# A transformer block on one core: a beta moved from VectorE to GpSimd, TensorE given idle transposes during the first load, and a new order of work

## The chip, the cores and the metric

The kernel runs on one core of a Trainium2 chip. Its engines are TensorE (PE; its weight loads are shown as PEld), VectorE (DVE), ScalarE (ACT), GpSimd (POOL) and SyncE (SP), which issues the DMAs. Times are device microseconds of one execution; the number to predict is the median over several executions.

## The reference

`x` holds 8 batches of 512 rows of 256 floats (fp32), `ctx` 64 rows per batch. Per batch:

```
y = ln0(x)                                        # no gain, no shift
y = ln(y + attention(y, y, y, causal), g1, beta1)
y = ln(y + attention(y, ctx, ctx),     g2, beta2)
h = relu(y @ w1 + b1)                             # 256 -> 1024
y = ln(y + h @ w2 + b2,                g3, beta3)
x = x + y
q = fp4(ln0(x))                                   # blocks of 16 quantised and scaled back
h = silu(q @ fp4(w_gate).T) * (q @ fp4(w_up).T)   # 256 -> 704
x = x + fp4(h) @ fp4(w_down).T
```

Keys and queries are the rows themselves; there are no projections. `beta3` is one row of 256 floats, added to all rows in the third norm. Since x + (norm * g3 + beta3) = (x + beta3) + norm * g3, it may be added to x at any time after `ln0(x)` has been taken.

## The kernel before, in words

Rows lie on the 128 partitions, so a batch is four row tiles of 128x256. All matmuls are fp32. Each stage of a batch is built from small operations that name an engine, a cost, the buffers they read and write, and what they emit (`Plan.op`, line 118). Nothing is emitted at once. At the end (L1171) `Plan.order` runs a list scheduler: every engine that is free takes the ready operation with the smallest key, provided that the buffers it needs can be had, and the instructions are emitted in that order. So each engine gets one fixed queue, worked off first to last, and an instruction whose input is late holds up all behind it.

The key comes from `_keys` (L153): the due time of the operation's batch and stage (the table `DUE`, L45) less the costs of what follows it. `push` shifts a key: `LOAD_EARLY` (L44) pulls the loads of x and z forward, and the weights (L1163) are pushed back. Costs and dues are constants in the file; what they say is only the planner's, and it acts on the chip through the order alone. The number of buffers of each kind (L310 to L347) also shapes the order.

Stages, with the lines whose instructions matter below:

- `load` (L349): x of a batch (L358, four DMAs for batch 0, else one of 512 KB) and z, that is `ctx`, twice (L366).
- `self_attention` (L747): `norm_stats` takes row statistics on VectorE (L448, L438, L439), 1/sqrt on GpSimd as a power (L458) and a shift on VectorE (L465); `layernorm` writes y on ScalarE, a row tile each (L524); `turned` transposes y on TensorE (L419) in two halves that ScalarE copies out of PSUM (L831); scores on TensorE (L767: for each of four key tiles two products, 512, 384, 256 and 128 columns wide); exp on ScalarE (L778); the causal mask as a select on GpSimd (L787); values on TensorE (L800); division on VectorE (L806, L807). `scaled_norm` (L531) takes squares on ScalarE (L488), the power on GpSimd (L503), gain and shift on VectorE (L537, L545).
- `cross_attention` (L860): z transposed (L419, copied at L867 into `zT`), the batch's result `r` transposed (L419, L831), keys (L883) copied as `kq` (L896) and transposed back (L900), exp (L890), values (L927).
- `mlp` (L947): up products (L961) with relu (L969), down products (L981). `by_row` (L552, its instruction at L557) adds `b2` to r and `beta3` to x on VectorE, four instructions of 128x256 each.
- `glu` (L1019): fp4 on VectorE and ScalarE (L578 to L610), gate and up products (L1036), down products (L1116), result stored (L1133).
- `columns` (L724) loads `b1` as eight rows, `c_rows`, which TensorE transposes (L733), and seven vectors spread over all partitions by DMA (L743). `pads` (L1146) stores a tile of zeros, `nothing`, into three DRAM buffers (L1149).

Before the plan begins, GpSimd makes the identity `ident` and fills the constant parts of 2 `y0`, 8 `z` and 3 `hqT` buffers and `nothing` (L374 to L388).

Of the kernel before, what the change touches and what calls it, by code (L numbers as in the profile page):

```python
# [14 lines left out]
ALU = mybir.AluOpType  # L15
# [23 lines left out]
TURN = 2.6  # L39

TILED = 2.65

BY_PRODUCTS = (4, 2, 1)
LOAD_EARLY = 2191.0  # L44
DUE = [  # L45
    [-1877.0, 638.0, 1236.0, -86.0, 359.0],
    [-498.0, 1140.0, 299.0, -53.0, 352.0],
    [251.0, 920.0, -109.0, 452.0, 665.0],
    [2244.0, 599.0, -92.0, 754.0, 95.0],
    [1032.0, 759.0, 1302.0, 1127.0, 22.0],  # L50
    [818.0, -579.0, 119.0, -1108.0, 586.0],
    [771.0, -1583.0, 341.0, 621.0, 85.0],
    [127.0, -388.0, -430.0, -94.0, -1479.0],
    [-2334.0],
]
# [205 lines left out]
def kernel(  # L261
# [51 lines left out]

    z_homes = several("z", 8, [P, D + 2])
    plan.kind("y0", y0_homes)
    plan.kind("z", z_homes)
    plan.kind("zT", several("zT", 6, [P, ND, SZ]))
    plan.kind("turned", several("turned", 3, [P, ND, S]), ordered=False)
    plan.share("y0T", "turned", 1)
    plan.share("yT", "turned", 3, ordered=False)  # L320
    plan.share("zqT", "turned", 3)
    plan.kind("e", several("e", 1, [P, NT * (NT + 1) // 2 * P]))
    plan.kind("r", several("r", 3, [P, NT, D]))
    plan.kind("kq", several("kq", 4, [P, S // 2]))
    plan.kind("xp", several("xp", 6, [P, NT, SZ]))
    plan.kind("xpT", several("xpT", 3, [P, NT // 2 * P]))
    plan.kind("hT", several("hT", 8, [P, S]))
    plan.kind("zq", several("zq", 1, [P, NT, D]))
    plan.kind("zm", several("zm", 2, [P, NT * D]), ordered=False)
    plan.kind("wide", several("h", 8, [P, NI * P]), ordered=False)  # L330
    plan.share("h", "wide", 5)
    plan.share("hm", "wide", 3)
    plan.share("wq", "wide", 7)
    hqT_homes = several("hqT", 3, [P, NI * P])
# [7 lines left out]
    plan.kind("zd", zd_homes, ordered=False)  # L342
    plan.kind("ln", several("ln", 12, [P, 48]), ordered=False)
    plan.kind("q", several("q", 6, [P, 3, 64]), ordered=False)
    plan.kind("rt", several("rt", 7, [P, 4]), ordered=False)
# [3 lines left out]
    def load(b):  # L349
        xs, zs = plan.buf("x"), plan.buf("z")  # L350
        plan.batch, plan.stage = b, 0
        plan.push = -LOAD_EARLY

        for ts_ in [[t] for t in range(NT)] if not b else [list(range(NT))]:
            lo, n = ts_[0], len(ts_)
            plan.op(
                "SP", 0.65 * n,
                lambda lo=lo, n=n: nc.sync.dma_start(  # L358
                    xs.ap[:, lo : lo + n, :],
                    x[b, lo * P : (lo + n) * P].rearrange("(t p) d -> p t d", p=P),  # L360
                ),
                writes=[(xs, t) for t in ts_],
            )
        for i in range(2):
            plan.op(
                "SP", 0.4, lambda i=i: nc.sync.dma_start(zs.ap[ts(i, SZ), :D], z[b]),  # L366
                writes=[(zs, i)],
            )
        plan.push = 0.0
        return xs, zs  # L370
# [3 lines left out]
    make_identity(nc, ident)  # L374
    for t in y0_homes:
        nc.gpsimd.memset(t[..., D:], 1.0)
    for t in z_homes:
        nc.gpsimd.memset(t[:, D:], 1.0)

    for t in hqT_homes:  # L380
        nc.gpsimd.memset(t[RI:, WI * P :], 0.0)
    squares = fixed("squares", [P, D])
    mhalf = fixed("mhalf", [P, NT])
# [3 lines left out]
    nothing = fixed("nothing", [P, 2, NI * P - I], U16)  # L387
    nc.gpsimd.memset(nothing, 0)  # L388

# [14 lines left out]

    plan.kind("const", ["const"] * 13, ordered=False)
    ready = {}
    for name in ("cols", "g1", "beta1", "g2", "g3", "beta2", "beta3", "b2", "w1", "w2", "wgu", "wd", "pads"):
        ready[name] = plan.buf("const")


    def transposed(blocks, src, dst, emit_evict, cost, width, also=()):

        pt = plan.buf("bank")

        def go():
            at = 0
            for blk in blocks():
                rows, n = blk.shape
                nc.tensor.transpose(pt.ap[:n, ds(at, rows)], blk, ident[:rows, :rows])  # L419
                at += rows  # L420

        plan.op("PE", 0.112 * width, go, reads=src, writes=[pt], takes=[dst[0]])
        plan.op("ACT", cost, lambda: emit_evict(pt.ap), reads=[pt, *also], writes=[dst])

    def norm_stats(v, view, pairs):
# [18 lines left out]
        for ts_ in pairs:  # L444
            lo, hi = ts_[0], ts_[-1] + 1
            for t in ts_:
# [9 lines left out]
            plan.op(  # L456
                "POOL", 1.05,
                lambda lo=lo, hi=hi: nc.gpsimd.tensor_tensor(  # L458
# [16 lines left out]
    def sums_stats(v, view, s):  # L475
# [9 lines left out]
        for t in range(NT):  # L485
            plan.op(
                "ACT", 0.52,
                lambda t=t: nc.scalar.activation(  # L488
                    squares, view(t), AF.Square, bias=s.ap[:, 24 + t : 25 + t],
                    accum_out=s.ap[:, 28 + t : 29 + t],  # L490
                ),
                reads=[(v, t), (s, t)], writes=[(s, ("sq", t))],
            )
# [7 lines left out]
        plan.op(  # L501
            "POOL", 1.05,
            lambda: nc.gpsimd.tensor_tensor(s.ap[:, 36:40], s.ap[:, 32:36], mhalf, ALU.pow),  # L503
            reads=[(s, "var")], writes=[(s, ("rstd", t)) for t in range(NT)],
        )

    def layernorm(dst, dview, v, view, s=None, pairs=(range(NT),)):

        if s is None:
            s = norm_stats(v, view, [list(ts_) for ts_ in pairs])  # L510
        else:
# [8 lines left out]
            )  # L520
        for t in range(NT):
            plan.op(
# [224 lines left out]
    def self_attention(b, xs):  # L747
# [4 lines left out]
            y0, lambda t: y0.ap[:, t, :D], xs, lambda t: xs.ap[:, t, :],  # L752
            pairs=(range(NT),) if b else (range(NT // 2), range(NT // 2, NT)),
        )
        yT = turned(y0, "y0T", b < BY_PRODUCTS[0], lambda t: y0.ap[:, t, :D])


# [3 lines left out]
        for k in range(NT):  # L761
# [3 lines left out]
            def scores(k=k, n=n, sc=sc):  # L765
# [19 lines left out]
            plan.op(  # L785
                "POOL", 0.35,
                lambda k=k: nc.gpsimd.affine_select(  # L787
# [7 lines left out]
        for t in range(NT):  # L795
# [9 lines left out]
            def divide(t=t, av=av, rt=rt):  # L805
# [7 lines left out]
                "PE", (t + 1) * pe(D + 2), product,  # L813
                reads=[(e, k) for k in range(t + 1)] + [(y0, k) for k in range(t + 1)],
                writes=[av], takes=[r],
# [6 lines left out]

    def turned(v, kind, by_products, view):

        yT = plan.buf(kind)
        if by_products:
            for c in range(ND):
                transposed(
                    lambda c=c: [view(t)[:, ts(c, P)] for t in range(NT)],
                    [(v, t) for t in range(NT)], (yT, c),  # L830
                    lambda pt, c=c: nc.scalar.copy(yT.ap[:, c, :], pt), act(S), NT,  # L831
                )
        else:
            turned_by_transfers(v, view, plan.buf("zm"), yT)
        return yT
# [111 lines left out]
    def mlp(b, r, xs):  # L947
# [5 lines left out]
        by_row(r, "b2", ALU.add)  # L953
        by_row(xs, "beta3", ALU.add)
        hT = []
        for f in range(NF):
            hp, h = plan.buf("bank"), plan.buf("hT")

            def product(f=f, hp=hp):
# [7 lines left out]
            plan.op(  # L967
                "ACT", act(S, True),
                lambda f=f, hp=hp, h=h: nc.scalar.activation(  # L969
# [49 lines left out]
    def glu(b, xs, s):  # L1019
# [91 lines left out]
        def last(t, hqT):  # L1111
            op = plan.buf("bank")

            def product(hqT=hqT, op=op):
# [6 lines left out]
            plan.op(  # L1121
                "PE", NI * pe(D), product, reads=[(hqT, 0), (hqT, 1), ready["wd"]], writes=[op]
            )
# [26 lines left out]


    columns()
    plan.op("SP", 3.5, pads, writes=[ready["pads"]])
    plan.batch = 0
# [7 lines left out]
    )  # L1162
    plan.push = 2035.0  # L1163
    weights()
# [40 lines left out]
```

## Time and profile before

| | us |
|---|---|
| median of 3 runs | 575.14 (575.07 to 575.2) |
| the profiled execution | 576.26 |
| its span, first to last instruction | 574.5 |
| TensorE matmuls busy | 563.8 |
| VectorE busy | 447.8 |
| ScalarE busy | 361.8 |
| GpSimd busy | 62.2, 93 instructions |

In the profile an fp32 matmul is two instructions, and a transpose is one. An instruction's duration includes the time it takes to drain, so in a full TensorE queue the step from one start to the next is shorter than the mean duration: 13.73 us for 32 L961 instructions, 0.43 each, whose mean duration is 0.59. For GpSimd, durations are rough. The chain that ended last is followed back from the last instruction, at each step to what released it. The granted TensorE clock is 1.00 in every stretch.

VectorE's 32 instructions that add `beta3` take 0.420 us each, 12.3 us busy in all. On GpSimd the 32 L503 powers take 1.18 us on average, 1.01 where nothing else disturbs them, and 32 selects 0.29 at the median, 1.68 at most.

### The profile page before, as it was taken

What the parts mean: (1) busy time and instruction counts of PE and PEld (TensorE: products, weight loads), DVE (VectorE), ACT (ScalarE), POOL (GpSimd) and SP (SyncE); (2) the same over time, 40 slices, a digit from 0 to 9 for tenths busy, and PEclk for the clock granted to TensorE, in tenths of its full rate; (3) what the DMA queues carried; (4) which work ended last, traced back from release to release, by engine and by line L of the source; (5) the groups of instructions that cost most, each with busy time, mean ns of one, the idle gap of its engine ahead of it and who ended that gap; (6) DMA issues with size and microseconds to landing.
All of it is one profiled execution on the core that took longest, in us unless ns stands there. A gap on an engine that the chain in (4) does not pass through costs nothing.

```text
span 574.5 us, 7037 instructions
## 1 busy us (share of the span) xinstructions
PE 563.8 (98%) x2209; PEld 391.2 (68%) x2209; DVE 447.8 (78%) x1125; ACT 361.8 (63%) x761; POOL 62.2 (11%) x93
## 2 busy tenths in 40 slices
PE   5999999999999999999999999999999999999997
PEld 2767584866747668658486667766765866877686
DVE  4789988869998865755259999978997656399892
ACT  4677869598887672791638558887845256364431
POOL 3521101011200120110101102210100000010000
PEclk9999999999999999999999999999999999999999
DMA  7770387246466513322023546585771421436501
GB/s 236 119 230 2 101 219 169 73 119 157 116 158 175 137 52 83 99 71 49 1 73 98 137 126 156 148 198 154 153 180 62 124 62 38 111 106 151 151 19 46
DMA packets 143220, 66.88 MB, mean 116 GB/s; under 512 B 107976, under 2 KB 142672, under 8 KB 143184
## 3 DMA queue, kind: packets, MB, share of 16 engines
q1 hardware_dynamic: 143184, 66.44, 45.4%
q8 instruction: 17, 0.28, 0.2%
q14 instruction: 19, 0.16, 0.1%
HBM read 10.42 MB, written 29.66 MB: 70 GB/s over the span
## 4 chain that ended last, share of the span: by engine, by line
PE 98%; ACT 1%; DMA 0%; SPq 0%; issue 0%; DVE 0%; ACTq 0%
PE bank L1036 27%; PE bank L981 19%; PE bank L961 19%; PE bank L1116 15%; PE bank L767 7%; PE bank L800 6%; PE bank L419 2%; PE bank L927 1%; PE bank L883 1%; DMA z<-in_ctx_dram 0%; ACT squares L488 0%; PE bank L900 0%; SPq L358 0%; ACT turned L831 0%; PE bank L1102 0%
## 5 line engine op out<-in xcount | busy, mean ns | idle before, releaser
L1036 PE MATMUL bank<-wgu,turned 128*128 128x352 f32 x512 | 157.5, 460 | 0.0
L1036 PEld LDWEIGHTS bank<-wgu,turned 128*128 128x128 f32 x512 | 96.3, 190 | 51.8 <-issue 1.7
L981 PE MATMUL bank<-w,hT 128*128 128x256 f32 x512 | 112.6, 379 | 0.0
L961 PE MATMUL bank<-turned,w 128*128 128x512 f32 x256 | 112.5, 593 | 0.0
L981 PEld LDWEIGHTS bank<-w,hT 128*128 128x128 f32 x512 | 97.0, 190 | 13.8
L1116 PE MATMUL bank<-wd,hqT 128*128 128x256 f32 x384 | 87.2, 380 | 0.0
L961 PEld LDWEIGHTS bank<-turned,w 128*128 128x128 f32 x256 | 48.2, 190 | 56.9 <-issue 51.7
L1116 PEld LDWEIGHTS bank<-wd,hqT 128*128 128x128 f32 x384 | 72.4, 190 | 14.2 <-issue 2.9
L503 POOL TENSOR_TENSOR ln<-ln,mhalf 128x4 f32<-128x4 f32 x32 | 37.7, 1180 | 352.0 <-DVE ln L496 352.0
L603 DVE SCALAR_TENSOR_TENSOR h<-h,h 128x704 f32<-128x704 f32 (+2 forms) x76 | 66.8, 883 | 3.8 <-ACT h L597 3.4
L488 ACT ACTIVATE squares<-r,ln 128x256 f32<-128x256 f32 x96 | 48.7, 508 | 32.0 <-DVE ln L480 29.7
L969 ACT ACTIVATE hT<-bank,cols 128x512 f32<-128x512 f32 x64 | 42.8, 681 | 21.7 <-PE bank L961 21.5
L1048 ACT ACTIVATE h<-bank 128x352 f32<-128x352 f32 x64 | 29.2, 460 | 36.4 <-PE bank L1036 32.5
L1071 ACT COPY h<-h 128x1408 uint16<-128x1408 uint16 x28 | 38.0, 1362 | 19.4 <-DVE h L610 17.9
L1055 DVE TENSOR_TENSOR h<-h,bank 128x352 f32<-128x352 f32 x64 | 32.4, 516 | 12.3 <-PE bank L1036 8.6
L992 DVE SCALAR_TENSOR_TENSOR r<-bank,r 128x256 f32<-128x256 f32 x32 | 13.5, 421 | 35.0 <-PE bank L981 34.7
L767 PE MATMUL bank<-turned 128*128 128x512 f32 (+3 forms) x128 | 39.8, 457 | 0.4 <-ACT turned L831 0.4
L597 ACT ACTIVATE h<-h 128x704 f32<-128x704 f32 (+2 forms) x38 | 29.7, 788 | 14.0 <-DVE h L591 13.9
L800 PE MATMUL bank<-y,e 128*128 128x258 f32 x160 | 36.8, 381 | 0.0
L800 PEld LDWEIGHTS bank<-y,e 128*128 128x128 f32 x160 | 30.1, 190 | 5.9 <-issue 1.0
L591 DVE SCALAR_TENSOR_TENSOR h<-h,q 128x704 f32<-128x704 f32 (+2 forms) x38 | 33.5, 883 | 0.2
L610 DVE TENSOR_TENSOR h<-h,q 128x704 f32<-128x704 f32 (+2 forms) x38 | 33.4, 879 | 0.2
(90 smaller groups left out, 639.9 us busy)
## 6 DMA issues: line engine op xcount, KB each, us to landing
zd<-zm SPq DMA_DIRECT2D x25, 512.0 KB, 3.0
hd<-h SPq DMA_DIRECT2D x30, 352.0 KB, 3.0
out_dram<-x SPq DMA_DIRECT2D x32, 128.0 KB, 1.7
x<-in_x_dram SPq DMA_DIRECT2D x7, 512.0 KB, 5.3
w<-in_L_xattn_w_dram SPq DMA_DIRECT2D x2, 1024.0 KB, 7.4
z<-in_ctx_dram SPq DMA_DIRECT2D x16, 64.0 KB, 4.6
zd<-h SPq DMA_DIRECT2D x2, 384.0 KB, 3.1
h<-in_L_ffn_w_down_dram SPq DMA_DIRECT2D x2, 352.0 KB, 4.2
```

The lines of the kernel that those rows point to most:

```text
L488: lambda t=t: nc.scalar.activation(squares, view(t), AF.Square, bias=s.ap[:, 24 + t : 25 + t], accum_out=s.ap[:, 28 + t : 29 + t],),
L503: lambda: nc.gpsimd.tensor_tensor(s.ap[:, 36:40], s.ap[:, 32:36], mhalf, ALU.pow),
L591: lambda: nc.vector.scalar_tensor_tensor(blocks_of(view()), blocks_of(view()), TIE, each(rc()), ALU.mult, ALU.mult),
L603: lambda reverse=reverse, f=f: nc.vector.scalar_tensor_tensor(view(), mm(), LEAST, view(), ALU.max, f, reverse1=reverse),
L767: nc.tensor.matmul(sc.ap[:, :n], yT.ap[:, c, ts(k, P)], yT.ap[:, c, k * P :], start=(c == 0), stop=(c == ND - 1),)
L800: nc.tensor.matmul(av.ap[:, : D + 2], e.ap[:, ds(start[k] + (t - k) * P, P)], y0.ap[:, k, :], start=(k == 0), stop=(k == t),)
L961: nc.tensor.matmul(hp.ap, w1_sb[:, c, ts(f, P)], yT.ap[:, c, :], start=(c == 0), stop=(c == ND - 1),)
L969: lambda f=f, hp=hp, h=h: nc.scalar.activation(h.ap, hp.ap, AF.Relu, bias=b1_sb[:, f : f + 1]),
L981: nc.tensor.matmul(fp.ap[:, :D], hT[f].ap[:, ts(t, P)], w2_sb[:, f, :], start=(f == 0), stop=(f == NF - 1),)
L1036: nc.tensor.matmul(gp.ap[:, :HI], zT.ap[:, c, ts(t, P)], wgu[:, c, ds(j * I + n * HI, HI)], start=(c == 0), stop=(c == ND - 1),)
L1071: lambda: nc.scalar.copy(planes(), h.ap[:, :I].bitcast(U16).rearrange("p (k h) -> p h k", h=2)),
L1116: nc.tensor.matmul(op.ap[:, :D], hqT.ap[:, ts(c, P)], wd[:, c, :], start=(c == 0), stop=(c == NI - 1),)
```

## The change

- **beta3**: `by_row(xs, "beta3")` on VectorE becomes four GpSimd instructions per batch on the same data.
- **Idle transposes**: 22 transposes of `ident` into a PSUM bank that nobody reads, first in TensorE's queue.
- **First rows on two engines**: for batch 0, y's row tiles 1 and 3 are written by VectorE (`tensor_scalar`), tiles 0 and 2 by ScalarE, and the second half of the transposed y is copied out of PSUM by VectorE.
- **Fills late**: only the first `y0` and the first `z` buffer are filled at once. The other fills and `nothing` become planned GpSimd operations with a late key, and their readers wait for them.
- **Durations**: the planner's costs of the power (1.05 to 1.12), the square (0.52 to 0.63), the select (0.35 to 0.44) and the relu (0.68 to 0.57) change.
- **Dues anew**: the table of dues, `LOAD_EARLY`, the push of the weights and the counts of some buffers (`kq` 4 to 1, `xp` 6 to 3, `xpT` 3 to 9, `hT` 8 to 9, `z` 8 to 9 and others) change.

```diff
-LOAD_EARLY = 2191.0
+LOAD_EARLY = 1813.0
 DUE = [
-    [-1877.0, 638.0, 1236.0, -86.0, 359.0],
+    [-1960.0, 1449.0, 703.0, -221.0, -105.0],
...
+    fills = [(of_y0, y0_homes[1:]), (of_z, z_homes[1:]), (of_hqT, hqT_homes)]
+    of_y0(y0_homes[0])
+    of_z(z_homes[0])
...
+        for t in on_dve:
+            plan.op(
+                "DVE", 0.35,
+                lambda t=t: nc.vector.tensor_scalar(
+                    dview(t), view(t), s.ap[:, 36 + t : 37 + t], s.ap[:, 40 + t : 41 + t],
+                    ALU.mult, ALU.add,
+                ),
...
-                    lambda pt, c=c: nc.scalar.copy(yT.ap[:, c, :], pt), act(S), NT,
+                    lambda pt, c=c: (
+                        nc.vector.tensor_copy(yT.ap[:, c, :], pt)
+                        if first and c
+                        else nc.scalar.copy(yT.ap[:, c, :], pt)
+                    ),
+                    act(S), NT, engine="DVE" if first and c else "ACT",
...
-        by_row(xs, "beta3", ALU.add)
+        for t in range(NT):
+            plan.op(
+                "POOL", 0.75,
+                lambda t=t: nc.gpsimd.tensor_tensor(
+                    xs.ap[:, t, :], xs.ap[:, t, :], vecs["beta3"][0], ALU.add
+                ),
+                reads=[(xs, t), ready["beta3"]], writes=[(xs, t)],
+            )
...
+    idle = plan.buf("bank")
+    def warm():
+        for _ in range(WARM):
+            nc.tensor.transpose(idle.ap[:, :P], ident, ident)
+    plan.op("PE", 0.22 * WARM, warm, writes=[idle])
     columns()
-    plan.op("SP", 3.5, pads, writes=[ready["pads"]])
+    plan.push = 2333.0
+    plan.op(
+        "POOL", 0.2, lambda: nc.gpsimd.memset(nothing, 0), writes=[(ready["fills"], "nothing")]
+    )
+    for fill, homes in fills:
+        for k, t in enumerate(homes):
+            plan.op(
+                "POOL", 0.45, lambda fill=fill, t=t: fill(t), writes=[(ready["fills"], (fill, k))]
+            )
...
-    plan.push = 2035.0
+    plan.push = 2333.0
     weights()
```

## The prediction

> **What bounds the kernel now.** I read the busy shares first, then the chain that ended last, then its first 60 us in order of time, then GpSimd's own timeline, then two-microsecond windows for the DMA rate. The page:
>
> ```profile
> PE 563.8 (98%) x2209; PEld 391.2 (68%) x2209; DVE 447.8 (78%) x1125; ACT 361.8 (63%) x761; POOL 62.2 (11%) x93
> PE 98%; ACT 1%; DMA 0%; SPq 0%; issue 0%; DVE 0%; ACTq 0%
> ```
>
> The first row is busy time, the second the chain by engine: TensorE is the bound. The view of waits gives it only 5.6, 0.9, 0.7 and 0.4 us of waiting, all before 36.9 us. So what can be won lies in the first 37 us. The chain there (start, length, what):
>
> ```profile
> 2.66 2.77 DMA z<-in_ctx_dram
> ...
> 8.33 1.74 PE bank L419 x7
> 10.06 6.71 PE bank L767 x16
> 16.78 4.36 PE bank L800 x20
> 21.14 1.14 PE bank L419 x10
> 22.28 4.11 PE bank L767 x12
> 26.39 0.15 PE bank L733
> 26.54 0.64 PE bank L767 x4
> 27.18 4.59 PE bank L800 x20
> 31.77 0.45 PE bank L419 x4
> ...
> 36.85 1.99 PE bank L767 x4
> ```
>
> The same 16 score matmuls cost 6.71 us for batch 0 and 4.11 + 0.64 = 4.75 for batch 1: half speed at the start, about 2 us lost. Transposes show it too: 1.74 / 7 = 0.25 us at 8.33, 0.45 / 4 = 0.11 at 31.77. Between 31.77 and 36.85 TensorE waits for ScalarE (squares, `kq`, `turned`).
>
> **The start: idle transposes, rows on two engines.** 22 transposes of `ident` begin when it is made (about 1.45 us) and cost 22 x 0.21 = 4.7 us cold, to 6.2. The z transposes, at 5.56 before, now come behind them, and ScalarE's `zT` copy, which stands ahead of y's rows in its queue, too: row 0 starts near 6.95 instead of 6.21. ScalarE then has two rows (2 x 0.52) instead of four, and VectorE the other two (0.42 each, from the 0.42 of a L557 row), so rows end at 8.05 instead of 8.27. Scores could start at about 9.4 instead of 10.0. VectorE's copy of the second half stands behind the statistics of batch 1's x, which wait for that x: it landed at 8.9 (the statistics start at 8.91) and they take 1.41, so 10.3 + 0.6 = 10.9. Cold, the first half's matmuls cover that (9.4 + 1.7 = 11.1).
>
> Does the clock come up? The row: half speed lasts till about 14.4 (the weight loads of L767 step by 0.85 us up to 13.57; ten of them fit into the 2.4 us after 14.21), 4.4 us after the first matmul at 9.99, though transposes ran without a pause from 8.33, which is 6.1 us earlier. The Trainium skill, "TensorE: Matmul & The Clock Gate", Part 4, says that transposes don't count as activity for the gate, and Part 1 that full speed comes about 4 us into sustained matmuls. Were transposes counted, 12.3 would have been expected. Row and rule speak against the warm-up. By the rule, batch 0's scores are cold again and its value products (L800) start at 9.4 + 6.7 + 0.15 + 0.22 = 16.5 instead of 16.78, as the transpose of `c_rows` and those of batch 1's z now stand between scores and values. If transposes count, scores wait for VectorE's copy at 10.9, run 3.5 us warm, and L800 starts at 14.9. I take 16.5.
>
> **Fills late.** The memsets (0.1 to 0.2 us each) run in GpSimd's idle time before its first power and between the first two. Nothing waits; 0. Dearest: one 0.2 in front of a power.
>
> **The queue of SP.** In the built order the three pad stores move up to right behind batch 1's x, and the seven vectors (g1 to beta3) ahead of x of batches 3 to 5 and of batch 2's z, whose transposes stand in front of batch 1's scores. The pads' own wait for the fill `nothing` ends before SP reaches them (about 1.6 against 4.5 us). Before, the vectors were on the way from 17 us on, and nobody waited for them:
>
> ```profile
> 18.00:20.00 2.00, 2.00 (x11) 1.74 (x10) 1.84 (x9) 0.56 (x2) 0.43 (x1) 1.00 0.76 136
> 20.00:22.00 2.00, 2.00 (x15) 1.65 (x14) 1.91 (x10) 0.39 (x1) 0.00 (x0) 1.00 0.87 129
> 22.00:24.00 2.00, 2.00 (x7) 1.00 (x7) 1.90 (x14) 1.94 (x7) 0.43 (x1) 1.00 1.34 78
> 24.00:26.00 2.00, 2.00 (x8) 1.33 (x7) 0.74 (x4) 1.97 (x7) 2.00 (x3) 1.00 0.65 99
> ```
>
> The last number is GB/s. The vectors are 7 x 131 = 917 KB; 2 us x (136 + 129 + 78 + 99) = 884 KB by 26, so they take some 8.3 us, far under the 315 GB/s of x at 10 to 12 us. Now they start when batch 2's x has landed: 8.9, pads and z about 1, 524 KB at 315 = 1.7, its late issue 1: near 12.5. So beta3 lands at about 12.5 + 8.3 + 0.5 for the last completion = 21.3 and that z just behind it (19 if the slow pace was the neighbours' fault). Batch 1's transposes end at 16.5 + 4.36 + 0.9 = 21.75 cold, 20.1 warm: z costs nothing cold and eats 1.4 warm. Scores of batch 1: 22.1 against 22.28. Batches 3 to 5 land near 27 instead of 17, still ahead of their readers but for one statistics instruction of batch 3, which waits in VectorE's queue till 23.6, before the squares are done.
>
> **beta3 on GpSimd.** VectorE loses 32 x 0.42 = 13.4 us; as TensorE never waits for VectorE after 37 us, that is worth 0. GpSimd gains 32 adds of 128x256. No row shows one. Below: a select of 128 columns with one input takes 0.29; twice the columns, 0.58. Above: GpSimd held up by VectorE:
>
> ```profile
> 25.53 1.01 POOL L503 TENSOR_TENSOR ln<-ln,mhalf 128x4 f32<-128x4 f32 x1
> 26.50 1.89 POOL L787 TENSOR_SCALAR_AFFINE_SELECT e<-e 128x128 f32<-128x128 f32 x4
> ...
> 40.14 1.68 POOL L787 TENSOR_SCALAR_AFFINE_SELECT e<-e 128x128 f32<-128x128 f32 x1 [2.53 <-ACT e L778]
> ```
>
> At 40.14 a 0.29 us select takes 1.68, beside seven L557 adds on VectorE. The skill's "SBUF — State Buffer", "Who interferes with whom", says either side may block, since a VectorE instruction with two SBUF inputs shares a read port with GpSimd; here VectorE's own L557 stay at 0.42, so by the row VectorE keeps its gain and GpSimd pays; by the rule VectorE could give back up to 32 x 0.58 = 19 us, which its 22% idle time covers. I take 0.85 for an add (the price in "GPSIMD Engine Reference", 3.1, 4.5 us for 2048 columns, is 0.56 plus dispatch, an estimate), bounds 0.58 to 1.7.
>
> What is queued behind them? GpSimd's order becomes: four selects of batch 0, a power, **six adds, which wait for beta3**, batch 0's power (`rstd`), then the selects of batch 1, which L800 of batch 1 waits for. Adds: 21.4 + 6 x 0.85 + 0.1 = 26.6; power 1.0; select 0.3: L800 of batch 1 starts at 27.95, against 27.18. At 0.58 the adds end at 25.0, the power then waits for ScalarE's squares (25.5) and L800 starts near 27.0: -0.2. At 1.3 it starts at 30.6: +3.4. I take +0.8.
>
> **The order on ScalarE and the rest of the dues.** After batch 0's `r` transposes, the copies ahead of `kq` grow by one `turned` (0.53) and two `zT` (0.45): `kq`'s transposes 5.4 us behind the `r` transposes instead of 4.4. The scores of batch 2 follow at 5.65 instead of 5.24, since their `turned` is copied earlier: +0.4. The 0.15 wait of the `r` transposes near 39.1 goes: more matmuls now stand ahead of them. From there both orders hold the same TensorE work. Followed by hand to batch 0's first L961, the new order shows no further wait; beyond it I take 0, up to 2 in places where a power stands behind adds, below -0.2 excluded, as TensorE has no waiting left to lose. The tail (3.2 us) is the same. The planner's four new durations and the buffer counts act through this order alone.
>
> **Sum.** +0.8 + 0.4 - 0.15 = +1.05. The profiled execution took 576.26, its span 574.5 and 1.8 around it, 1.1 above the median 575.14. Span 575.55, profiled 577.3, median **576.2 us**.
>
> **The rivals.** (a) The start carries through: transposes count, the vectors land by 19, the adds are done before the squares. Then L800 of batch 1 starts at 25.5, -1.7; +0.4 - 0.15 leave 573.7. For it: cold matmuls do cost 2 us. Against: gate row, DMA rate. It decides on whether beta3 lands before 19.5, and is the one that ends faster. (b) The adds cost 0.6 to 0.7 and hide behind the squares: 575.1 to 575.6, no change. For it: GpSimd is 11% busy. (c) Adds beside VectorE's two-input runs take 1.3 or more, and batch 1 alone loses 3.4: 578.8. For it: the 1.68.
>
> **How the numbers follow.** Likeliest case 0.48 (575.6 to 578), (b) 0.27, (a) 0.15, (c) 0.10. A measurement here tells 0.2%, 1.15 us, from no change. The likeliest case lies astride the bound, 576.29: slower 0.34 of it, same 0.14; (a) faster 0.11, same 0.04; (c) slower. Faster 0.11, same 0.45, slower 0.44. The range for 8 in 10 is 574.2 to 578.5.
>
> **What would show it.** Right: batch 0's first score matmuls step by 0.85; six GpSimd adds start near 21.5 and end after 26; L800 of batch 1 waits for a select; scores of batch 2 start near 38; no TensorE wait beyond 40. Wrong: score steps of 0.43 from the start, beta3's first add before 19, adds of 0.6, or waits of TensorE for GpSimd or VectorE after 40 us.

## The result and the profile after

| | before | after |
|---|---|---|
| median, us | 575.14 (575.07 to 575.2) | 581.76 (579.35, 581.76, 582.0) |
| ratio, 95% interval | | 1.010 (1.0085 to 1.0116) |
| the profiled execution | 576.26 | 582.0 |
| its span | 574.5 | 580.3 |
| GpSimd busy | 62.2 | 90.2 |

The changed kernel is slower by 1.0%, where 576.2 us were forecast. In the line numbers of after, L785 are the scores, L818 the values, L805 the selects, L562 the shift of a norm, L427 transposes, L920 the copy of `kq`, L608, L620 and L627 the fp4 steps, L1067 and L1147 the gate, up and down products of `glu`, L1108 the store of hd, L981 the beta3 adds, L1189 the idle transposes.

The first two lines of the page after that answer to the two shown of before, busy time and the chain that ended last:

```profile
PE 568.0 (98%) x2231; PEld 394.8 (68%) x2231; DVE 443.5 (76%) x1096; ACT 360.7 (62%) x758; POOL 90.2 (16%) x126
PE 86%; DMA 7%; DVE 4%; SPq 1%; POOL 1%; issue 1%; POOLq 0%
```

TensorE's share is unchanged at 98%; the idle transposes are 5.0 us of its time, and its total grew by 4.2. The second row tells more: the chain was TensorE to 98%, and now DMAs and VectorE hold 11% of it. VectorE lost 32 adds that were 12.3 us busy, yet its busy time fell by only 4.3. Eight microseconds came back, 1.5 of them in the two rows and the copy of batch 0, the rest in instructions that take longer.

What TensorE waited for (total, times, longest):

```profile
PE bank L1147 <- DMA hqT<-hd: 3.1, 3, 1.8
PE bank L1189 <- POOL ident masks.py:199: 1.4, 1, 1.4
PE bank L924 <- ACT kq L920: 1.4, 1, 1.4
PE bank L818 <- POOL e L805: 1.2, 1, 1.2
...
PE bank L785 <- DMA turned<-zd: 0.5, 1, 0.5
PE bank L427 <- DVE r L562: 0.5, 1, 0.5
```

The first, but for 0.2 us, and the fifth of these lie at 326, 345 and 362 us, in a stretch in which TensorE did not wait at all before. The chain there (start, length, what):

```profile
317.22 6.80 DMA hd<-h
...
324.04 3.96 DMA hqT<-hd
...
328.13 2.83 PE bank L1147 x12
330.96 8.37 PE bank L1067 x28
339.33 2.67 PE bank L1147 x12
...
342.44 4.05 DMA hqT<-hd
...
358.62 4.44 DMA turned<-zd
```

Three transfers come too late for TensorE. To put a number on each place I pair the two traces at equal amounts of TensorE work, idle transposes left out, and subtract the times: this is how far after lies behind before. It is -1.5 us at 25 us, -0.45 at 31, +1.22 at 60, +1.29 at 315, +5.53 at 375, +5.75 at the end. So the start, in which the whole forecast lay, ends 1.2 us behind, and 4.5 us are lost later, nearly all of it between 320 and 365 us. Both traces are of slow runs of their kernel (576.26 against a median of 575.14, 582.0 against 581.76), so lags hold for these runs, and the table below has the medians. Below, "late loss" is what is lost from 60 us to the end.

What VectorE does there, before and after, in the windows of all engines (PE, PEld, DVE, ACT, POOL busy, clock, DMA share, GB/s):

```profile
315.00:325.00 10.00, 10.00 (x35) 6.40 (x35) 9.93 (x22) 7.12 (x12) 1.51 (x1) 1.00 0.48 135
325.00:335.00 10.00, 10.00 (x41) 7.39 (x40) 9.38 (x19) 3.06 (x7) 0.00 (x0) 1.00 0.33 86
345.00:355.00 10.00, 10.00 (x40) 6.95 (x39) 9.90 (x28) 7.21 (x13) 1.63 (x2) 1.00 0.71 170
```

```profile
315.00:325.00 10.00, 10.00 (x36) 6.40 (x35) 6.94 (x15) 5.64 (x10) 0.66 (x1) 1.00 0.57 142
325.00:335.00 10.00, 8.19 (x31) 5.52 (x30) 9.87 (x16) 5.89 (x9) 8.32 (x5) 1.00 0.35 89
345.00:355.00 10.00, 8.93 (x34) 6.09 (x33) 9.61 (x22) 6.42 (x9) 0.75 (x1) 1.00 0.47 142
```

The first fence is before: VectorE, 78% busy over the span, is 94 to 99% busy in this stretch. It is a second bound, with no room. After, it stands still for 3 us at 320, and is full again with fewer instructions done: 16 in place of 19 at 325 to 335, beside 8.3 us of GpSimd.

### The profile page after: what moved, and what is told of

It is laid out like the page before. It is cut to its first block, busy times and chain, and to the rows that moved or that the text cites. A ratio compares the mean times of both kernels' runs of the same rounds, so it can differ in the third digit from the quotient of the medians.

```text
span 580.3 us, 7092 instructions
## 1 busy us (share of the span) xinstructions
PE 568.0 (98%) x2231; PEld 394.8 (68%) x2231; DVE 443.5 (76%) x1096; ACT 360.7 (62%) x758; POOL 90.2 (16%) x126
## 4 chain that ended last, share of the span: by engine, by line
PE 86%; DMA 7%; DVE 4%; SPq 1%; POOL 1%; issue 1%; POOLq 0%
PE bank L1067 23%; PE bank L992 19%; PE bank L1012 18%; PE bank L1147 14%; PE bank L818 4%; PE bank L785 4%; DMA hqT<-hd 2%; DMA x<-in_x_dram 2%; PE bank L951 1%; PE bank L907 1%; DVE r L562 1%; DMA hd<-h 1%; DMA v_beta<-in_L_xattn_beta_dram 1%; PE bank L427 1%; DMA turned<-zd 1%; DVE ln L456 1%
## 5 line engine op out<-in xcount | busy, mean ns | idle before, releaser
L1067 PE MATMUL bank<-wgu,turned 128*128 128x352 f32 x512 | 157.4, 460 | 0.0
L1067 PEld LDWEIGHTS bank<-wgu,turned 128*128 128x128 f32 x512 | 96.3, 190 | 52.6 <-issue 2.4
L1147 PE MATMUL bank<-wd,hqT 128*128 128x256 f32 x384 | 87.6, 381 | 3.1 <-DMA hqT<-hd 3.1
L1147 PEld LDWEIGHTS bank<-wd,hqT 128*128 128x128 f32 x384 | 72.2, 190 | 17.8 <-ACT zm L614 2.3
L620 DVE SCALAR_TENSOR_TENSOR h<-h,h 128x704 f32<-128x704 f32 (+2 forms) x76 | 68.0, 897 | 6.5 <-ACT h L614 6.3
L785 PE MATMUL bank<-turned 128*128 128x512 f32 (+3 forms) x128 | 38.1, 443 | 0.5 <-DMA turned<-zd 0.5
L818 PE MATMUL bank<-y,e 128*128 128x258 f32 x160 | 37.1, 383 | 1.2 <-POOL e L805 1.2
L595 DVE TENSOR_REDUCE q<-h 128x44 f32<-128x704 f32 (+2 forms) x38 | 33.3, 877 | 2.9 <-DMA h<-in_L_ffn_w_up_dram 2.6
L818 PEld LDWEIGHTS bank<-y,e 128*128 128x128 f32 x160 | 29.9, 190 | 7.4 <-POOL e L805 1.8
L608 DVE SCALAR_TENSOR_TENSOR h<-h,q 128x704 f32<-128x704 f32 (+2 forms) x38 | 34.5, 910 | 0.2
```

The costliest lines, as they stand in the source:

```text
L608: lambda: nc.vector.scalar_tensor_tensor(blocks_of(view()), blocks_of(view()), TIE, each(rc()), ALU.mult, ALU.mult),
L620: lambda reverse=reverse, f=f: nc.vector.scalar_tensor_tensor(view(), mm(), LEAST, view(), ALU.max, f, reverse1=reverse),
L785: nc.tensor.matmul(sc.ap[:, :n], yT.ap[:, c, ts(k, P)], yT.ap[:, c, k * P :], start=(c == 0), stop=(c == ND - 1),)
L818: nc.tensor.matmul(av.ap[:, : D + 2], e.ap[:, ds(start[k] + (t - k) * P, P)], y0.ap[:, k, :], start=(k == 0), stop=(k == t),)
L1067: nc.tensor.matmul(gp.ap[:, :HI], zT.ap[:, c, ts(t, P)], wgu[:, c, ds(j * I + n * HI, HI)], start=(c == 0), stop=(c == ND - 1),)
L1147: nc.tensor.matmul(op.ap[:, :D], hqT.ap[:, ts(c, P)], wd[:, c, :], start=(c == 0), stop=(c == NI - 1),)
```

## The experiments

Theory A: GpSimd's adds cost the time. They hold back the queue in batch 0 and stretch VectorE's instructions where VectorE is full. Theory B: the new order costs it, by batch 6's load of x above all. Every kernel was timed beside the kernel before on its own chip; the table has both medians. In kernels that only leave out, swap or move instructions, the order of all others is that of the kernel they are made from.

| kernel | us | before beside it | ratio (95%) |
|---|---|---|---|
| after again, two groups | 580.63; 580.49 | 575.8; 575.55 | 1.0086; 1.0091 (1.007 to 1.011) |
| e1 no adds | 575.6 | 575.28 | 1.0008 (0.9997 to 1.0018) |
| e2 adds on VectorE | 580.41 | 575.28 | 1.0087 (1.007 to 1.0104) |
| e3, e13 no idle transposes | 578.66; 579.11 | 575.28; 575.55 | 1.0061; 1.006 (1.0046 to 1.0076) |
| e4 before, adds on GpSimd | 577.36 | 575.28 | 1.0039 (1.0024 to 1.0054) |
| e6 x of batch 6 early | 578.44 | 575.8 | 1.0049 (1.0034 to 1.0064) |
| e7 no adds of batches 6, 7 | 578.61 | 575.8 | 1.0062 (1.0042 to 1.0083) |
| e9 no adds of batches 0 to 5 | 577.27 | 575.6 | 1.003 (1.0018 to 1.0042) |
| e10 e6 and e7 together | 577.72 | 575.6 | 1.0046 (1.0032 to 1.0061) |
| e8 before, the change's start | 575.26 | 575.8 | 0.9999 (0.9989 to 1.0009) |
| e11 e8, `kq` copied earlier | 575.35 | 575.6 | 1.0002 (0.9993 to 1.0011) |
| e12 before, idle transposes | 575.89 | 575.6 | 1.0005 (0.9995 to 1.0016) |

### The adds left out, and put back on VectorE

```diff
-                lambda t=t: nc.gpsimd.tensor_tensor(
-                    xs.ap[:, t, :], xs.ap[:, t, :], vecs["beta3"][0], ALU.add
-                ),
+                lambda: None,                                        # e1
+                lambda t=t: nc.vector.tensor_tensor(                 # e2
+                    xs.ap[:, t, :], xs.ap[:, t, :], vecs["beta3"][0], ALU.add
+                ),
```

> The changed kernel with its 32 beta3 additions left out and nothing in their place (beta3 is not added to x); every other instruction stays in its place on its engine. Theory A, the additions on GpSimd cost the time (they stretch VectorE's two-input steps and hold back power and selects in batch 0): all three late waits of TensorE (1.97, 1.24 and 0.67 us) and about 1.5 us of the start go, and the time is 575 to 577 us. Theory B, the new order costs it (x of batch 6 is asked for 2.9 us later and its transfer holds back the store of hd behind it and VectorE behind x): the wait of 1.97 us at 326 us stays, and the time is 578.5 to 580.5 us.

575.6 us, 0.3 over the kernel before beside it, and no wait of TensorE after 60 us. Theory B by itself, which wanted 578.5 to 580.5, falls: of the 4.8 us that after was over before when run again, 4.5 go with the adds. Without the adds, everything else in the change sums to 0.3 us (-0.2 to 1.0), no measurable difference. That does not make the new order free with them: see e4, e6 and e13.

> The changed kernel with the 32 beta3 additions carried out by VectorE at the same point of the order (all else in place). Theory A: the four additions beside batch 6's block steps then cost VectorE 4 x 0.34 = 1.4 us in place of about 2 us of stretched steps, and batch 0's power starts at once; 579.5 to 581 us, a little under the changed kernel, with VectorE's L620 back at 0.88 us throughout. Theory B: the same as the changed kernel within 1 us, with the wait at 326 us whole. If VectorE keeps its gain from the move, as the prediction took it, this one is slower than the changed kernel by up to 1 us.

580.41 us: in this order the adds are as dear on VectorE as on GpSimd, though not at the same places. L620 on 704 columns is back at 0.88 us, and the late loss is 2.04 against after's 4.53. But this trace is 2.84 us behind at 60 us, where after is 1.22: TensorE waits 2.6 us for `kq` in place of 1.4, and then the granted clock, the number before the last two, is half for 3.4 us:

```profile
38.20:41.50 3.30, 3.30 (x6) 1.44 (x5) 3.07 (x9) 2.74 (x9) 1.19 (x2) 0.50 0.05 15
```

All four runs of e2 have a mean granted clock of 0.996 or 0.997, which is what one such stretch makes of 580 us; of the seven of after and e5 three have it, of the twelve of e1 two. So the move won VectorE nothing that the kernel could use; nor did it lose against this version. That the two totals agree is in part chance.

### The adds alone, in the order of before

```diff
-        by_row(xs, "beta3", ALU.add)
+        by_row(xs, "beta3", ALU.add, nc.gpsimd)
```

> The kernel before with its 32 beta3 additions on GpSimd instead of VectorE, everything else in place (the order is not made anew). The prediction's sum for this step alone: +0.8 us at batch 1's values and nothing later, 575.5 to 576.3 us. Theory A: the additions also stretch VectorE's two-input steps wherever they lie beside them; 577 to 579.5 us, with some late waits of TensorE for hqT or for x. Theory B: the additions alone do little, 575 to 576 us, and no late wait of TensorE for hqT.

577.36 us, 2.1 over before: in theory A's range, not in that of the prediction's own sum for this step, nor of B. But the late waits that A also expected are not there. By the trace the loss is at one place: this kernel is 0.47 us ahead of before's trace at 31 us, 1.00 behind at 50, and 1.05 at the end. GpSimd and VectorE of this kernel:

```profile
36.70 4.89 POOL L557 TENSOR_TENSOR x<-x,v_beta 128x256 f32<-128x256 f32 x6
36.75 3.56 DVE L545 SCALAR_TENSOR_TENSOR r<-r,ln,v_beta 128x256 f32<-128x256 f32 x4 [0.29 <-POOL ln L503]
```

The same four L545 in the kernel before:

```profile
37.64 1.67 DVE L545 SCALAR_TENSOR_TENSOR r<-r,ln,v_beta 128x256 f32<-128x256 f32 x4 [0.23 <-POOL ln L503]
```

Four instructions take 3.56 us in place of 1.67, because six adds run beside them: 0.89 each instead of 0.42. TensorE's transposes of `r` wait for each pair, 0.76 us twice, counted from where the next would have started. After has the same at the same place:

```profile
37.88 3.12 DVE L562 SCALAR_TENSOR_TENSOR r<-r,ln,v_beta 128x256 f32<-128x256 f32 x4 [0.57 <-POOL ln L511]
```

There the waits are 0.65 and 0.32 us. In the old order, then, the adds on GpSimd cost 2.1 us, in the new one 4.5 (e1): the rest is what the adds and the new order, its start included, cost together.

### The two late causes, one at a time and both

The instructions in question are left out or moved and the rest stays; e5 is the kernel after once more. Line numbers of e6 and e10 are two higher.

```diff
+    xs.home = fixed("x_extra", [P, NT, D])      # e6, e10: x of batch 6 in a buffer of its own
+    first = sp[sp.index(o6) - 3]                # its load three places up in SP's queue
+    out_.remove(o6)
+    out_.insert(out_.index(first), o6)
...
-                lambda t=t: nc.gpsimd.tensor_tensor(
+                lambda t=t: b >= 6 or nc.gpsimd.tensor_tensor(     # e7, e10; e9: b < 6
```

> The changed kernel unaltered, beside the kernels of this group. Its first three times spread over 2.7 us (579.35 to 582.0). If the wait at 326 us depends on how long the store of zd ahead of it takes (4.7 us in the first trace, 2.9 to 3.5 us in two kernels without the wait), the times spread again, 579 to 582.5 us, and a trace with a short store has a shorter wait there.

580.63 us, runs from 579.75 to 581.24. The store of zd took 4.7 us again, the store of hd 5.7 instead of 6.8, VectorE stood still for 1.84 us, and the late loss was 3.65.

> The changed kernel with x of batch 6 loaded into a buffer of its own, asked for three places earlier in SP's queue, while the DMA engines are idle. Theory B (the late load holds back the store of hd behind it and VectorE behind x): the store of hd takes under 3.5 us in place of 6.8, VectorE's idle stretch of 2.8 us at 320 us goes, TensorE waits at 326 us no more and at 345 and 362 us by less than 0.5 us in sum: 577.5 to 578.5 us. Theory A (the additions of batches 6 and 7 stretch VectorE's steps by 3.2 us where it is full): only the wait at 326 us goes, the waits at 345 and 362 us keep 1.5 us or more: 579 to 580.5 us.

578.44 us, 2.2 less than after beside it. SP's queue in after, from the store of zd on (the transposing load L1113 cannot start before the store of hd has landed):

```profile
314.55 1.95 SPq L878 DMA_TRANSPOSE turned<-zd  x1
316.54 0.58 SPq L360 DMA_DIRECT2D x<-in_x_dram  x1
317.22 0.56 SPq L1108 DMA_DIRECT2D hd<-h  x1
324.04 1.42 SPq L1113 DMA_TRANSPOSE hqT<-hd  x1
```

And in e6:

```profile
314.54 2.06 SPq L880 DMA_TRANSPOSE turned<-zd  x1
316.69 0.56 SPq L1110 DMA_DIRECT2D hd<-h  x1
320.32 1.41 SPq L1115 DMA_TRANSPOSE hqT<-hd  x1
```

The 512 KB of x in front of it had made hd's 352 KB land after 6.80 us instead of 3.6, and VectorE, whose next instruction was the statistics of that x, had waited for it. Both are gone, and so is the wait at 326. After 60 us the view of waits has 0.6 us left, and the late loss is 1.33. The time is in B's range and below A's: the adds alone do less than A had it.

> The changed kernel without the eight beta3 additions of batches 6 and 7 (for those two batches beta3 is not added to x); the 24 others stay on GpSimd, everything in its place. Theory A: VectorE gets 3.2 us of stretching back, the waits at 345 and 362 us go, and of the one at 326 us at most what the store of hd makes; 577 to 579 us. Theory B: the waits stay as in the changed kernel, within 1 us of it.

578.61 us, 2.0 less than after beside it; late loss 0.25, although the load of x is where it was: here A is right. (The trace is of its fastest run, 577.6; its slowest took 580.37 and has no trace.) The same VectorE instructions in after and in e7, first after, with GpSimd's line ahead of them (each start, length):

```profile
328.53 6.48 POOL L981 TENSOR_TENSOR x<-x,v_beta 128x256 f32<-128x256 f32 x4 [0.91 <-ACT y L541]
...
328.53 1.22 DVE L620 SCALAR_TENSOR_TENSOR zq<-zm,zq 128x1024 f32<-128x1024 f32 x1
329.67 1.42 DVE L608 SCALAR_TENSOR_TENSOR h<-h,q 128x704 f32<-128x704 f32 x1
331.01 1.75 DVE L620 SCALAR_TENSOR_TENSOR zq<-zm,zq 128x1024 f32<-128x1024 f32 x1
...
334.34 1.41 DVE L620 SCALAR_TENSOR_TENSOR h<-h,h 128x704 f32<-128x704 f32 x1
```

```profile
325.81 1.22 DVE L620 SCALAR_TENSOR_TENSOR zq<-zm,zq 128x1024 f32<-128x1024 f32 x1
326.95 0.89 DVE L608 SCALAR_TENSOR_TENSOR h<-h,q 128x704 f32<-128x704 f32 x1
327.75 1.22 DVE L620 SCALAR_TENSOR_TENSOR zq<-zm,zq 128x1024 f32<-128x1024 f32 x1
...
330.35 0.89 DVE L620 SCALAR_TENSOR_TENSOR h<-h,h 128x704 f32<-128x704 f32 x1
```

0.89 becomes 1.42, 1.22 becomes 1.75: half a microsecond on an instruction that reads two tiles of SBUF. Small ones that read one are stretched too at times: an L602 of 44 columns takes 0.71 us once, 0.18 as a rule. GpSimd pays as well: these four adds take 1.4 to 1.8 us each, and 0.72 beside VectorE instructions that read one tile or PSUM. Eight adds stretched VectorE by 3.2 us; on VectorE they would have taken 8 x 0.34 = 2.7 us of its queue.

> The changed kernel without the 24 beta3 additions of batches 0 to 5 (there beta3 is not added to x); the eight of batches 6 and 7 stay on GpSimd, everything in its place. With all additions left out the kernel took 575.6 us, with only the early ones kept 578.6, unaltered 580.6. If early and late additions cost separately (theory A), this one takes 577 to 578.3 us, with waits of TensorE between 325 and 365 us as in the changed kernel (2 us or more in sum) and its values of batch 1 no longer behind a select. If the late waits only come about because the start ran late, the late waits are under 1 us and the time is 575.5 to 576.5 us.

577.27 us over eight runs. The late waits are there in full without the early adds, so the late part is no consequence of the start. This trace is of a run of 579.85, one of its two slowest; the median is 2.6 us shorter, and how much of that is late is not shown:

```profile
PE bank L1147 <- ACT zm L614: 1.2, 1, 1.2
PE bank L1147 <- DMA hqT<-hd: 1.1, 1, 1.1
PE bank L785 <- DVE q L603: 0.8, 1, 0.8
```

And this trace lies 0.98 us ahead of before at 60 us, where after is 1.22 behind. So the 24 early adds cost 2.2 us by these traces; by the medians, each less its own before, 4.83 (after again) - 1.67 = 3.2. The trace of e1, whose first 60 us are the same program, gives less: it is 1.89 ahead at 31 us but 0.14 behind at 60, as four of its scores run at half speed again (see the last section). The early share is known to about 1 us, no better.

> The changed kernel with both late causes taken away: x of batch 6 asked for early into a buffer of its own, and the eight additions of batches 6 and 7 left out (there beta3 is not added to x). Each alone gave 578.4 and 578.6 us. If the two overlap (VectorE takes either into its slack, not both), this gives hardly more: 577.8 to 578.6 us, and no late wait. If they add up, 576.4 us.

577.72 us: 0.5 under e6 and 0.7 under e7 by the same reckoning, so the two causes overlap more than they add. The traces of all kernels in this order of work show how (e2's adds are on VectorE itself):

| trace | adds of 6, 7 beside VectorE | VectorE stands still for x | late loss |
|---|---|---|---|
| after; e9; e5 | yes | 2.83; 2.30; 1.84 | 4.53; 4.59; 3.65 |
| e14; e3; e13; e6 | yes | 0.72; 0.18; 0; 0 | 1.20; 1.19; 1.17; 1.33 |
| e2 | on VectorE | 1.67 | 2.04 |
| e7; e1; e10 | no | 0.35; 0; 0 | 0.25; 0.28; 0.50 |

The adds alone cost about 0.9 us (1.2 against 0.25 to 0.5); from 1.8 us of standing still on, beside the adds, 3.7 to 4.6 are lost. No trace has a long standstill without the adds, so what a late x costs alone is not shown.

### The start

```diff
-    plan.op("PE", 0.22 * WARM, warm, writes=[idle])
+    plan.op("PE", 0.22 * WARM, lambda: None, writes=[idle])   # e3, e13
```

> The changed kernel without its 22 idle transposes. As the prediction took it (they do not count for the clock): nothing changes, batch 0's scores are as in the changed kernel and its values start at 15.2 us. If they do bring up the clock: the scores run at half speed again until about 4 us after the first transpose of y, batch 0's values start at 16.4 to 16.8 us, and what is left of that at the end is 0 to 1.2 us: 581.8 to 583.2 us.

578.66 us, and neither expectation fits: less than after, where equal or more was expected. Values of batch 0 start at 14.9 us, with the scores' half speed ending near 11.1.

> The changed kernel without its idle transposes, a second time, now beside the changed kernel on the same chip. The first time it took 578.66 us, 2 us less than the changed kernel in another group. If the idle transposes bring the later steps into a worse place (the store of zd at 309 us then ends just as the store of x behind it begins, lands after 4.7 us instead of 2.9, and x of batch 6 comes later), it is again 1.5 to 2.5 us faster than the changed kernel, with zd landed after about 2.9 us and under 1 us of wait at 326 us in its trace. If the 2 us lay in the chip or the group, the two agree within 0.5 us.

> The changed kernel unaltered, on the same chip as the one without idle transposes. 580 to 581.5 us, if it repeats; the store of zd at 309 us lands after 4.7 us, and TensorE waits 3 us or more between 325 and 365 us.

579.11 (578.46 to 579.19) against 580.49 (578.51 to 582.75) on the same chip: 1.4 us less, a little under the 1.5 to 2.5 expected. The 2 us did not lie in the chip. The store of zd at 310 us lands after 2.9 us in both traces without idle transposes and after 4.6 to 5.0 in seven of the nine of this order that have them, e14 among them (3.5 in e1 and e7). The old order shows the same: 3.0 and 2.9 in before and e4, 4.6 to 4.8 in e8, e11 and e12.

What ties the first 6 us to this store is a queue that fetches instructions. The page after has it:

```profile
q8 instruction: 17, 0.28, 0.2%
```

That is 17 transfers of 16 KB. From one to the next TensorE starts 253 matmuls and weight loads on average (218 to 283), so I take them for its own. The 22 transposes are 44 instructions more, and the tenth transfer comes at 312.4 us in after and 311.8 in e14, at 320.3 in e13 and 320.0 in e3. The queues while the store of zd was under way, in after (309.76 to 314.48) and in e13 (310.33 to 313.23):

```profile
q1 hardware_dynamic: 672, 0.66, 42.2%
q8 instruction: 1, 0.02, 1.2%
```

```profile
q1 hardware_dynamic: 528, 0.52, 53.5%
```

In all 16 traces this store lands within 3.04 us where no transfer of q8 starts in its first 3 us (four traces), and after 3.5 to 5.0 where one does (twelve). Over all stores of zd of 512 KB with a landing in these traces the medians are 3.0 us (310 stores) and 4.6 (36). The store's own data have been moved 2.5 us after its issue in after as in e13; why the landing waits is not shown, and no run moved a fetch alone. The trace of e14, its quickest run, shows that the store does not decide by itself: zd took 4.7, but hd only 4.5, and TensorE waited just 0.9 us in the view of waits, where 3 had been expected.

```diff
+    for _ in range(22):                                        # e8, e11, e12: ahead of all else
+        nc.tensor.transpose(banks[7][:, :P], ident, ident)
...
+                lambda t=t: (nc.vector.tensor_scalar(          # e8, e11: rows 1 and 3 of batch 0
...
+                lambda pt, c=c: (nc.vector.tensor_copy if first and c else nc.scalar.copy)(
...
+    before, behind, last = near(-1), [near(1), near(2)], near(4)   # e11: kq's copy up, zT's down
```

> The kernel before with the change's start alone, nothing else moved: 22 idle transposes first on TensorE, rows 1 and 3 of batch 0's first layernorm and its second turned copy on VectorE; beta3 stays on VectorE, and the order is not made anew. As the prediction took it, the idle transposes do nothing and the time is that of before, 575.0 to 575.6 us. If they bring up the clock, batch 0's values start 1.2 to 1.8 us earlier; with the start carried through 573.5 to 574.2 us, with batch 1's scores waiting for their data as they do before, 574.6 to 575.4 us.

575.26 against 575.8; the ratio says no difference. In the trace batch 0's values start at 15.3 instead of 16.6, after a wait of 1.35 us for the select, and at 60 us the kernel is 1.24 us ahead of before's trace. That trace is one of the slower executions of before (576.26 against medians of 575.1 to 575.8), so about 0.5 us is what the medians leave. And the lead does not last: it is 1.08 at 325 us and 0.33 from 375 us on, after a wait of 0.51 us for `turned` at 366 that before does not have.

> The kernel before with 22 idle transposes first on TensorE and nothing else. If they bring up the clock, the scores of batch 0 step by 0.43 us per 512 columns from their start or from 10.5 us at the latest (as in the kernels with them so far), and batch 0's values start at 15.0 to 15.9 us instead of 16.6; the time is 574.6 to 575.6 us. If they do nothing, the scores are cold until about 14 us and the values start at 16.5 us or later, behind z's transposes; 575.3 to 576 us.

575.89, no difference; the values start at 16.0, 0.6 us earlier. The trace records the granted clock as full from 6.33 us, as the idle transposes end, half from 9.74, after TensorE's waits for y, and full again from 13.15: the warm-up was lost before the scores began. Nine of the twelve runs have a mean granted clock of 0.997 or less. This trace loses its 0.6 us between 315 and 325 us, with 0.47 of it in one wait of TensorE.

> The kernel before with the change's start (idle transposes, two rows and one copy of batch 0 on VectorE), and in ScalarE's queue batch 0's copy of kq one place earlier, ahead of the last square, and the two zT copies behind the two turned copies; beta3 stays on VectorE. TensorE waits 0.83 us for kq and 0.54 us for turned without that. If the waits end where those copies stood, 0.5 to 0.9 us come off: 574.3 to 574.8 us where before takes 575.3. If the power behind the squares and the r transposes of batch 1 take the wait over, it stays at 575.0 to 575.5 us.

575.35, no difference from before or from e8. TensorE's wait for `kq` is gone, and 0.70 us for `turned` stands in its place; at 60 us this trace is 1.76 ahead. Its span is 1.5 us shorter than before's; of that, 1 us is lost outside the span, in this run alone. I found no version that beats the kernel before by what can be measured.

## Why the prediction was wrong

**"By the row VectorE keeps its gain and GpSimd pays"** is the first step that failed. The row was a select held up by L557 adds that stayed at 0.42 us. A select reads one tile; an add on GpSimd reads two. L562 beside selects in after is hardly longer (0.50 against 0.48); beside adds it is 0.95. The nearest row was of the right engine and the wrong operation. In after, the instructions beside the adds are 8.4 us longer than their like, of 32 x 0.34 = 10.9 us of VectorE's queue that the move set free. The Trainium skill's "SBUF — State Buffer", "Who interferes with whom", which the prediction set aside for that row, was right that either side may block; the prediction's estimate from it, up to 19 us, was over twice what is measured.

**"Which its 22% idle time covers"** and **"as TensorE has no waiting left to lose"** are the second step, and the dearer one: an average over the span took the place of the stage. VectorE's 22% are elsewhere. In 305 to 365 us it was 94 to 99% busy before. "Beyond it I take 0, up to 2" should have been costed there: measured 4.5 in the profiled execution, and e6, e7 and e10 give its two parts. With the adds on VectorE, e2's late loss is still 2.04, so the room in its queue had to be looked up there, not the stretching alone.

**The queue of SP** was followed to batch 5's x and no further. What it missed is x of batch 6: asked for at 316.5 us, 0.7 ahead of a store of hd, where before x was asked for at 313.7 and the store came at 317.5, as x landed. e6 is worth 2.2 us.

**+0.8 at batch 1's values**: right in mechanism, wrong in sign. GpSimd's timeline in after:

```profile
20.38 4.71 POOL L981 TENSOR_TENSOR x<-x,v_beta 128x256 f32<-128x256 f32 x6 [0.57 <-DMA v_beta<-in_L_xattn_beta_dram]
25.19 1.19 POOL L511 TENSOR_TENSOR ln<-ln,mhalf 128x4 f32<-128x4 f32 x1
26.36 1.40 POOL L805 TENSOR_SCALAR_AFFINE_SELECT e<-e 128x128 f32<-128x128 f32 x4
```

Six adds ahead of the power, which is ahead of the selects: the adds began at 20.4 instead of 21.4 and took 0.785 each instead of 0.85, and the values started at 26.7 instead of 27.95, against 27.18 before. TensorE had arrived earlier and waited 1.35 us for the select. So the adds took back part of what the start had won. Without them e9 keeps 1 us at 60 us; e1 keeps none, for the half speed named under e9.

**"Row and rule speak against the warm-up"**, by which the idle transposes were to do nothing, was wrong. Batch 0's values started at 15.2 us in after, where 16.5 had been taken. Scores were fast from 10.5 us in after, 1.0 us after their first, and in five other traces of this order from the start. The rule taken from the Trainium skill's "TensorE: Matmul & The Clock Gate", Part 4, that transposes don't count, does not hold here. What they won at the start is little: e8 and e12 show nothing measurable, e12 because the clock mostly falls again. But as part of this change they cost 1.4 us (e13 beside e14), by the traces on a path that the forecast did not have: the fetch that meets the store of zd.

**+0.4 for `kq`** was +0.67 (waits of 1.50 against 0.83 in starts of instructions; 1.4 and 0.7 in the view of waits). **-0.15 for the `r` transposes** became +0.8, by the same stretching as in e4. By 60 us the terms, -0.5 and +1.7, gave +1.22 where +1.05 had been summed: right by chance.

**Rival (c)**, adds beside VectorE's two-input runs at 1.3 us or more, named the mechanism, with 0.10. It had the place wrong (batch 1, where they took 0.72 to 0.91) and left out VectorE's own share of the price.

## What to carry to other kernels

Moving work from a full engine to an idle one was not free where both read SBUF: side by side, two-input instructions took 0.5 us longer on VectorE and 0.9 to 1.8 us instead of 0.72 on GpSimd, and each add that saved 0.34 us of VectorE gave 0.26 back on average. Before writing "its idle time covers it", take the windows of the stage in which the moved work will lie; an engine at 78% over the span may have no room where it matters. And when an order is made anew, follow every big load to what stands just behind it in the queue, to the last batch. Instructions added at the start can also act far from it: here 44 of them shifted a fetch of instructions at 320 us by 8 us.

## What was not expected of the hardware

The clock comes up at different times in executions of one program, and transposes count. TensorE's start in e1, where the idle transposes themselves end at full speed, and in after, where even y's transposes are at half speed:

```profile
1.42 4.06 PE L1187 MATMUL bank<-ident 128*128 128x128 f32 x22 [1.42 <-POOL ident masks.py:199]
...
6.60 1.36 PE L427 MATMUL bank<-ident,y 128*128 128x128 f32 x8 [0.85 <-ACT y L541]
```

```profile
1.42 4.96 PE L1189 MATMUL bank<-ident 128*128 128x128 f32 x22 [1.42 <-POOL ident masks.py:199]
...
7.63 2.03 PE L427 MATMUL bank<-ident,y 128*128 128x128 f32 x8 [0.85 <-ACT y L541]
```

In e1 the step falls from 0.213 to 0.109 us at 4.4 us, in e5, the program of after, at about 6, in after at 10.5. The traces' records of the granted clock begin at these places: full from 4.41, 6.17 and 10.69 us, and from 14.47 in before. Ahead of the first record the profile's windows read 1.00, so the 1.00 of before says nothing of its first 14 us; half speed is seen there in the steps alone. The clock also goes down again: in e1, after 1.4 us of waiting for `kq`, four score matmuls from 35.1 us on stepped by 0.81 to 0.85 us once more, and here the windows show it:

```profile
35.20:38.50 3.30, 3.30 (x6) 1.24 (x5) 2.10 (x5) 2.34 (x8) 0.75 (x1) 0.50 0.85 260
```

The records have half clock from 35.13 to 38.54 us in e1, from 38.15 to 41.57 in e2, from 9.74 to 13.15 in e12: 3.41 us each time. From the first rise to the fall it is 30.72, 27.30 and 3.41 us, nine, eight and one times 3.41. Part 1 of the Trainium skill's "TensorE: Matmul & The Clock Gate" speaks of a window that runs freely of the program; these three traces agree: within an execution the clock changes at whole windows, and where they lie differs from one to the next.

The landing of a store goes with what other queues do. The same 512 KB store of zd at about 310 us landed after 2.9 to 3.0 us in the four traces in which no fetch of instructions fell into its first 3 us, and after 3.5 to 5.0 in the twelve in which one did.
